# A fused two-block kernel: the order of the second attention's steps, where the last scan's inputs stand, and the order of the W_dt products

## The chip, the cores and the metric

The kernel runs on one core of one Trainium2 chip. The time is the device time of one execution in microseconds (us), the median of three runs. A core has five engines with queues of their own: TensorE (PE: matrix products and transposes into PSUM), VectorE (DVE), ScalarE (ACT), GpSimd (POOL) and SyncE (SP, which here only issues transfers). ACT and POOL issue transfers too. SBUF and PSUM are the core's memories; what does not fit goes through DRAM.

## The reference

Four parts, each added to x, for 4 sequences of 512 tokens of 512 channels: causal attention with 16 heads; a feed-forward layer with ternary weights; a state-space scan; and a block of latent attention with mixture-of-experts. Cut to the parts that the change touches:

```python
x = x + attn0(layernorm(x));  x = x + ternary_ffn(layernorm(x))

u = layernorm(x)                                  # the scan
xz = u @ W_xproj.T                                # delta_r (128), B (16), C (16)
delta = softplus(delta_r @ W_dt.T + b_dt)         # (4, 512, 512)
dA = exp(delta[..., None] * -exp(A_log))          # 16 states per channel
Bu = delta[..., None] * B[:, :, None, :] * u[..., None]
h_t = dA_t * h_{t-1} + Bu_t;   y_t = sum(h_t * C_t, -1)
x = x + y + u * D_param

n = rmsnorm(x, ln1_w)                             # the second attention
kv, qd = n @ kv_d_w, n @ q_d_w                    # latents of 128
k, q, v from kv, qd and rotary parts; 16 heads of 32
probs = softmax(causal(q @ k.T / sqrt(32)))
h = x + (probs @ v) @ o_w
out = h + moe(rmsnorm(h, ln2_w))                  # 7 routed experts, top 2, and a shared one
```

## The kernel before

P = 128 rows is the unit; a sequence b (0 to 3) is four blocks of 128 tokens (NT) and four blocks of 128 channels (NK). The program runs in stages one after the other on the same core: first attention (to about 390 us of the profile), feed-forward (to 755), scan (to 1116), second attention (1163 to 1567, with an entry before it), experts (to the end). Within a stage, work of the next stage is woven in as Python generators, of which each `next` emits one part.

**Feed-forward.** PE's order is written out by hand (`manual_schedule`); the other engines' order is the framework's. For each block of hidden rows PE makes the gate and up products (`pg`, L819) and later the down products (`y`, L837). While sequence b is in the feed-forward, `prepare(b - 1)` makes the scan's inputs of the sequence before. In it, the step size is softplus of a product with W_dt: four products of 128x512 into the tile `pz` (L606), two halves of one PSUM pair each time. ACT reads each for |z| (`e`), DVE for max(z, 0) (`delta`, L608). A half is one part of the generator, so blocks of the feed-forward stand between the halves. The finished `delta`, and `dx` = delta times u turned to rows of tokens, are stored to DRAM (`deltas`, `dxs`).

**Scan.** 128 steps m: for each b, state n (16) and half of the channels. All five engines' orders are written out by hand. `scale(b, n)` loads a diagonal matrix (`diag_l`) on SP's queue, scales three token blocks of dx with B_n on ACT (`bu`, L1016) and makes four exponentials on ACT (`da`, L1022). `turn` forms the transposed inputs in PSUM on PE (L1029, L1034), `scan` runs two 512-long scans on DVE (L1042), `weigh` loads a row of C to all partitions (`cb`, SP's queue) and multiplies on POOL (`hc`, L1053, 128x1024), `add_up` adds up over n on PE (L1066). The pool `large` has two buffers of `delta_l` and `dxT`; `fetch(b)` fills one from DRAM in four parts, each with one load of `dxT` and one of `delta_l` of 256 KB, on SP's queue.

For the last sequence `prepare_last` makes the inputs during the scan itself, one part at each odd step from m = 5; its last parts copy each block on ACT from PSUM to a small tile and store it from ACT's queue. At m = 84 what is left of it is emitted, its pool is closed, and in the room of that pool come tiles for later (`ln2`, `wr`, `br` loaded at once). Then `fetch(B - 1)` starts, one part a step, and from m = 88 one weight load a step is issued from the list `loads` (`ln1`, `wlat`, `wrk` and others). At m = 100, 102, 104, 106 POOL scales a 128x256 block of `wlat` and one of `wrk` by `ln1` (L1164). From m = 86 `come` emits the entry of sequence 0 into the second attention at every third step; its root-mean-square helper is at L102.

**Second attention.** L1382 runs over m, 32 pairs of heads and query blocks for each sequence (b, group g of four heads, query block t, pair p). PE's order is written out, the others' is the framework's. The functions of a step:

- `soften(m)`: scores of two heads on PE (`scd`, L1303, one of two PSUM pairs), causal mask and negated row maximum on DVE (`nm`, L1311), two exponentials with row sums on ACT (`pr`, L1314).
- `turn`: t + 1 transposes for each head on PE (`tpd`, L1326), copied from PSUM by DVE for the first head (`ptd`, L1331) and by ACT for the second (L1333).
- `weigh`: for four heads the product of turned probabilities and values on PE (`avd`, L1344); after the last t, DVE multiplies by the inverted sums.
- `widen_sums`, `invert`: reciprocal on DVE, widened on ACT (`wide`, L1359), four transposes on PE (`tpr`, L1369) and a copy on ACT.
- fillers: parts of `leave` (output projection, residual and norm of the sequence before) and `enter` (latents, projections and rotary parts of the next).

A step emits soften(m), turn(m-2), at even m weigh of the two pairs m-4 and m-3, then fillers.

Of the kernel before, what the change touches and what calls it, by code (L numbers as in the profile page):

```python
# [19 lines left out]
P = 128  # L20
# [26 lines left out]
def block_kernel(ctx: ExitStack, tc: tile.TileContext, a: dict, out: bass.AP):  # L47
# [449 lines left out]
    large = scans.enter_context(tc.tile_pool(name="large", bufs=2, reuse_waits="tile"))  # L497
    loaded = {}

    def fetch(b):  # L500

        delta = large.tile([P, NK, T], F32, tag="one", name="delta_l")
        dxT = large.tile([P, NT, C], F32, tag="two", name="dxT")
        loaded[b] = delta, dxT
        for i in range(NT):
            nc.sync.dma_start(dxT[:, i, :], by_tokens(dxs, b)[:, i, :])
            nc.sync.dma_start(delta[:, i, :], by_rows(deltas[b])[:, i, :])
            yield
# [45 lines left out]
    def prepare(b, pool, spot, spots, ahead):  # L554


        x = xs[b]
        uT = pool.tile([P, NK, T], F32, tag="uT", name="uT")
        ops, rows = [], {}
        layer_norm(pool, x, lambda t, op: ops.append(op))  # L560
        yield

        def make(t):
            row = rows[t] = pool.tile([P, C], F32, tag="row", name="row_s", bufs=ahead)
            ops[t](row)
            ud = pool.tile([P, C], F32, tag="u", name="ud")
            nc.gpsimd.tensor_tensor(ud, row, dpar, ALU.mult)
            nc.gpsimd.tensor_tensor(x[:, t, :], x[:, t, :], ud, ALU.add)

        make(0)  # L570
        make(1)
        yield
        for t in range(NT):
            transpose_into(uT, rows.pop(t), t * P, spot=spot)
            if t == 1:
                make(2)
                make(3)
            yield
        pd = spot("pd")
        for k in range(NK):  # L580
            nc.tensor.matmul(pd, wx[:, k, :RANK], uT[:, k, :], start=k == 0, stop=k == NK - 1)
            if k == 1:
                yield
        drT = pool.tile([P, T], F32, tag="drT", name="drT")
        nc.scalar.copy(drT, pd)
        yield
        pb = spot("pb")
        latents(pb, uT)
        bcT = pool.tile([P, P], F32, tag="bcT", name="bcT")
        nc.scalar.copy(bcT, pb[:, :P])  # L590
        keep_latents(b, bcT, nc.sync)
        yield
        pb = spot("pbt")
        nc.tensor.transpose(pb[:, :P], bcT, ident)
        e = pool.tile([P, NK, T], F32, tag="e", name="diag_s")
        nc.sync.dma_start(diags[b], keep_inputs(b, pb, e))
        yield
        yield


        delta = pool.tile([P, NK, T], F32, tag="delta", name="delta")
        e = pool.tile([P, NK, T], F32, tag="e", name="e")
        for half in range(2):
            for i, pz in enumerate(spots("pz")):
                k = 2 * half + i
                nc.tensor.matmul(pz, wdt[:, k * P : (k + 1) * P], drT, start=True, stop=True)  # L606
                nc.scalar.activation(e[:, k, :], pz, AF.Abs, bias=bdt[:, k : k + 1])
                nc.vector.tensor_scalar(delta[:, k, :], pz, bdt[:, k : k + 1], 0.0, ALU.add, ALU.max)  # L608
            yield half == 1
        nc.scalar.activation(e, e, AF.Exp, scale=-1.0)  # L610
        yield True
        for k in range(NK):
            u = pool.tile([P, T], F32, tag="u", name="u")
            nc.vector.tensor_scalar(u, e[:, k, :], 1.0, -1.0, ALU.add, ALU.add)
            nc.vector.tensor_tensor(u, e[:, k, :], u, ALU.subtract)
            nc.vector.tensor_tensor(delta[:, k, :], delta[:, k, :], u, ALU.add)
            yield True
        nc.scalar.activation(e, e, AF.Ln, bias=1.0)
        yield True
        scaled = {}  # L620

        def finish(k):
            nc.vector.tensor_tensor(delta[:, k, :], delta[:, k, :], e[:, k, :], ALU.add)
            nc.sync.dma_start(deltas[b, k * P : (k + 1) * P, :], delta[:, k, :])
            scaled[k] = pool.tile([P, T], F32, tag="ux", name="ux", bufs=2)
            nc.vector.tensor_tensor(scaled[k], delta[:, k, :], uT[:, k, :], ALU.mult)

        def turn_out(k):
            tp, ux = spot("tpd"), scaled.pop(k)
            for t in range(NT):  # L630
                nc.tensor.transpose(tp[:, t * P : (t + 1) * P], ux[:, t * P : (t + 1) * P], ident)
            st = pool.tile([P, NT, P], F32, tag="st", name="st")
            nc.scalar.copy(st.rearrange("p t q -> p (t q)"), tp)
            nc.sync.dma_start(by_tokens(dxs, b)[:, :, k * P : (k + 1) * P], st)

        finish(0)
        yield True
        finish(1)
        yield
        for k in range(NK):  # L640
            turn_out(k)
            if k + 2 < NK:
                yield True
                finish(k + 2)
            yield

    def prepare_last(b, pool):
# [70 lines left out]
        for t in range(NT + 1):  # L718
            if t > 0:
                nc.vector.tensor_tensor(x[:, t - 1, :], x[:, t - 1, :], y, ALU.add)  # L720
            if t < NT:
                y = bank("du")
                for k in range(NK):
                    nc.tensor.matmul(
                        y[:, k * P : (k + 1) * P], uT[:, k, t * P : (t + 1) * P], dd[:, k, :],
                        start=True, stop=True,
                    )
                yield
        terms = ((ident, relu), (ident, e), (minus, over), (ident, ln))
        scaled = tp = None  # L730
        for k in range(NK + 2):
            if k >= 2:
                st = pool.tile([P, NT, P], F32, tag="st", name="st")
                nc.scalar.copy(st.rearrange("p t q -> p (t q)"), tp)
                nc.scalar.dma_start(by_tokens(dxs, b)[:, :, (k - 2) * P : (k - 1) * P], st)
            if 1 <= k <= NK:
                delta = pool.tile([P, T], F32, tag="delta", name="delta", bufs=2)
                nc.scalar.copy(delta, pd)
                nc.scalar.dma_start(deltas[b, (k - 1) * P : k * P, :], delta)
                scaled = pool.tile([P, T], F32, tag="ux", name="ux", bufs=2)  # L740
                nc.vector.tensor_tensor(scaled, pd, uT[:, k - 1, :], ALU.mult)
            if k < NK:
# [254 lines left out]
    with tc.tile_pool(name="c_1", bufs=1, reuse_waits="tile") as c1, tc.tile_pool(  # L997
# [83 lines left out]
        with tc.manual_schedule(engines=engines):  # L1081
# [4 lines left out]
            for m, (b, n, half) in enumerate(steps):  # L1086
# [27 lines left out]
                if m == 84:  # L1114
# [3 lines left out]

                    far = ctx.enter_context(tc.tile_pool(name="far", bufs=1, side="right"))
                    ln2 = far.tile([P, C], F32, tag="ln2", name="ln2")  # L1120
                    nc.sync.dma_start(ln2, a["ln2_w"].partition_broadcast(P))

                    wr = far.tile([P, NK, RW], F32, tag="wr", name="wr")
                    nc.gpsimd.memset(wr, 0.0)
                    nc.sync.dma_start(wr[:, :, :NR], by_rows(a["router_w"]))
                    br = far.tile([P, NR], F32, tag="br", name="br")
                    nc.sync.dma_start(br, a["router_b"].partition_broadcast(P))
                    logit = far.tile([P, TT, NR], F32, tag="logit", name="logit")

                    hs = [far.tile([P, NT, C], F32, tag=f"h{b}", name=f"h{b}") for b in range(B)]  # L1130
# [22 lines left out]
                    cos1 = held("cos1", [P, NT, RD], a["cos1"].rearrange("(t p) d -> p t d", p=P))  # L1153
                    sin1 = held("sin1", [P, NT, RD], a["sin1"].rearrange("(t p) d -> p t d", p=P))
                    wow = held("wow", [P, NK, C], by_rows(a["o_w"]))
                    coming = fetch(B - 1)
                if m >= 84:
                    next(coming, None)
                if m >= 88 and loads:
                    loads.pop(0)()  # L1160
                if 100 <= m < 100 + 2 * NK and m % 2 == 0:
                    k = (m - 100) // 2
                    for w in (wlat[:, k].rearrange("p i r -> p (i r)"), wrk[:, k]):
                        nc.gpsimd.tensor_scalar(w, w, ln1[:, k : k + 1], None, ALU.mult)  # L1164
            for step in steps[-3:]:
                add_up(*step)
            finish(B - 1)
# [58 lines left out]
    with tc.tile_pool(name="d_1", bufs=1) as d1, tc.tile_pool(name="d_2", bufs=2) as d2, tc.tile_pool(  # L1226
# [68 lines left out]
        def soften(b, g, t, p):  # L1295
# [13 lines left out]
            )  # L1309
            nm = d3.tile([P, 2], F32, tag="nm", name="nm")  # L1310
            nc.vector.tensor_reduce(nm, sc[:, :, :w], AX.X, ALU.max, negate=True)  # L1311
            pr = d3.tile([P, 2, T], F32, tag="pr", name="pr")
            for i in range(2):
                nc.scalar.activation(  # L1314
                    pr[:, i, :w], sc[:, i, :w], AF.Exp, bias=nm[:, i : i + 1],
# [57 lines left out]
        with tc.manual_schedule(engines={mybir.EngineType.PE}):  # L1373
# [2 lines left out]
            left = iter(())  # L1376
            n = len(pairs)
            each = n // B
            for m in range(n + 3):
                b, at = divmod(m, each)  # L1380
                if m < n:
                    soften(*pairs[m])  # L1382
                if 1 <= m < n + 1 and pairs[m - 1][2:] == (NT - 1, 1):
                    widen_sums(*pairs[m - 1][:2])
                if 2 <= m < n + 2:
                    turn(*pairs[m - 2])
                if 2 <= m < n + 2 and pairs[m - 2][2:] == (NT - 1, 1):
                    invert(*pairs[m - 2][:2])
                if m >= 4 and m % 2 == 0:
                    weigh(*pairs[m - 3][:3])  # L1390

                if m == (B - 1) * each:
                    fetch_shared()
                if m >= each and at == 2:
                    left = leave(b - 1, outs[b - 1])
                if at >= 3:
                    next(left, None)
                if at == 7:
                    come = enter(b + 1, d2) if b + 1 < B else iter(())
# [337 lines left out]
```

## Time and profile before

| | us |
|---|---|
| median of three runs | 1910.6 (1908.81 to 1911.85) |
| the profiled execution | 1912.04 |
| its span | 1910.3 |
| feed-forward, 390 to 755: PE busy | 335.1 of 365 |
| scan, 755 to 1116: PE, DVE, ACT, POOL busy | 317.3, 320.4, 308.2, 311.7 of 361 |
| second attention, 1163 to 1567: PE busy | 378.7 of 404 |
| experts, 1567 to 1910: PE busy | 336.1 of 343 |

The profile is one execution; the span goes from its first to its last recorded instruction. A row of the page's fifth part reads: line, engine, operation, output tile <- input tiles, shape, count, then busy time, mean duration in ns of one, and the idle time just before such instructions with what ended it. A row of waits reads: who waited, for whom, us in total, how often, the longest. Names like `SPq` mean an engine's queue of transfers. What a stage is worth is read from its own window, since each has another limit:

```profile
PE   7999999999999988988988888999999999999998
DVE  6456445656564636998979856475565663422222
ACT  2433433333242436989977956566676662111111
POOL 2221212120202020989868940100001000144431
```

These are busy tenths in 40 equal slices of the span, 47.8 us each. The scan is slices 16 to 23, where POOL's row is high.

### The profile page before, as it was taken

The page shows a single profiled execution, that of the slowest core. Times are in us where ns is not written, and L with a number is a line of the kernel's source. Part 1 is how long each engine was busy: PE and PEld are TensorE (multiplying, and loading weights), DVE is VectorE, ACT ScalarE, POOL GpSimd, SP SyncE. Part 2 cuts the span into 40 slices and gives each one's busy share as a digit, 9 for nine tenths or more (in the row PEclk, how much of TensorE's full clock was granted, in tenths as well). Part 3 has the DMA queues.
Part 4 walks back from the last instruction along what each step waited for, and adds up shares of the span by engine and source line. Part 5 has one row for each costly group of instructions (what it writes and reads, how often), then busy time and mean ns, then how long its engine had stood idle before and what let it go on. Part 6 is the DMA issues. An engine that isn't in the chain of part 4 may idle for free. (4 is left out here: it accounts for less than half of the span.)

```text
span 1910.3 us, 27470 instructions
## 1 busy us (share of the span) xinstructions
PE 1767.4 (93%) x10374; PEld 1089.5 (57%) x10374; DVE 1119.4 (59%) x1812; ACT 937.5 (49%) x1932; POOL 575.0 (30%) x391
## 2 busy tenths in 40 slices
PE   7999999999999988988988888999999999999998
PEld 3433343437766666878877764555555554554444
DVE  6456445656564636998979856475565663422222
ACT  2433433333242436989977956566676662111111
POOL 2221212120202020989868940100001000144431
PEclk9999999999999999999999988999999999999999
DMA  7002200102010202332234200000001005545545
GB/s 250 8 1 89 82 1 1 45 1 78 1 56 34 89 23 78 96 112 81 70 127 125 62 6 1 1 10 14 1 23 34 23 7 179 196 89 89 93 81 139
DMA packets 78470, 119.27 MB, mean 62 GB/s; under 512 B 9802, under 2 KB 37066, under 8 KB 77780
## 3 DMA queue, kind: packets, MB, share of 16 engines
q1 hardware_dynamic: 66148, 92.97, 15.1%
q0 software_dynamic: 8656, 20.32, 6.0%
q10 hardware_dynamic: 3536, 4.23, 0.7%
q8 instruction: 83, 1.36, 0.3%
q14 instruction: 47, 0.39, 0.1%
HBM read 85.12 MB, written 35.52 MB: 63 GB/s over the span
## 5 line engine op out<-in xcount | busy, mean ns | idle before, releaser
L1053 POOL TENSOR_TENSOR hc<-h,cb 128x1024 f32<-128x1024 f32 x128 | 301.1, 2406 | 112.6 <-DVE h L1042 94.1
L1042 DVE TENSOR_TENSOR_SCAN h<-da,bu 128x512 f32<-128x512 f32 x256 | 291.2, 1199 | 26.1 <-PE bu L1034 13.1
L284 PE MATMUL pq<-wqkv,hT 128*128 128x512 f32 x384 | 179.4, 615 | 1.8 <-ACT hT L133 1.8
L1022 ACT ACTIVATE da<-delta_l,am 128x511 f32<-128x511 f32 x256 | 163.9, 709 | 6.7 <-DVE h L1042 6.7
L1314 ACT ACTIVATE pr<-scd,nm 128x128 f32<-128x128 f32 (+3 forms) x256 | 133.2, 528 | 56.1 <-DVE nm L1311 53.5
L819 PE MATMUL pg<-hTh,w 128*128 128x512 f32 (+1 forms) x352 | 146.3, 416 | 2.4 <-DVE sil L825 1.7
L1066 PE MATMUL ys<-ident,hc 128*128 128x128 f32 x1024 | 138.6, 279 | 6.9 <-POOL hc L1053 4.0
L819 PE MATMUL pg<-hTl,w 128*128 128x512 f32 (+1 forms) x352 | 140.1, 398 | 0.2 <-DVE hTl L807 0.2
L1034 PE MATMUL bu<-ident,bu 128*128 128x128 f32 x768 | 133.2, 281 | 7.5 <-ACT bu L1016 7.5
L1616 PE MATMUL pgr<-wgu,gTe 128*128 x304 | 137.1, 593 | 0.0
L1016 ACT ACTIVATE bu<-dxT,bts 128x512 f32<-128x512 f32 x192 | 124.3, 711 | 23.1 <-PE bu L1034 21.2
L1029 PE MATMUL bu<-diag_l,dxT 128*128 128x128 f32 x512 | 108.7, 295 | 27.1 <-DVE h L1042 15.3
L364 ACT ACTIVATE pt<-sc 128x1024 f32<-128x1024 f32 (+3 forms) x128 | 84.1, 698 | 85.0 <-PE sc L359 82.6
L284 PEld LDWEIGHTS pq<-wqkv,hT 128*128 128x128 f32 x384 | 71.4, 194 | 94.4 <-issue 84.8
L1066 PEld LDWEIGHTS ys<-ident,hc 128*128 128x128 f32 x1024 | 119.7, 144 | 9.5 <-POOL hc L1053 5.9
L1303 PE MATMUL scd<-qkTd 32*128 32x512 f32 (+3 forms) x512 | 106.9, 496 | 13.7 <-ACT pr L1314 12.7
L1029 PEld LDWEIGHTS bu<-diag_l,dxT 128*128 128x128 f32 x512 | 81.3, 198 | 48.1 <-DVE h L1042 26.9
L1311 DVE TENSOR_REDUCE nm<-scd 128x2 f32<-128x256 f32 (+3 forms) x128 | 104.2, 815 | 0.0
L1326 PEld LDWEIGHTS tpd<-ident,pr 128*128 128x128 f32 x640 | 68.8, 142 | 60.2 <-issue 41.6
L1034 PEld LDWEIGHTS bu<-ident,bu 128*128 128x128 f32 x768 | 96.5, 146 | 11.5 <-ACT bu L1016 11.4
L365 POOL TENSOR_SCALAR_AFFINE_SELECT pt<-pt 128x512 f32<-128x512 f32 x64 | 43.5, 679 | 197.0 <-ACT pt L364 197.0
L1326 PE MATMUL tpd<-ident,pr 128*128 128x128 f32 x640 | 100.3, 288 | 0.6 <-ACT pr L1314 0.6
(310 smaller groups left out, 3184.9 us busy)
## 6 DMA issues: line engine op xcount, KB each, us to landing
cb<-c_rows SPq DMA_DIRECT2D x64, 256.0 KB, 3.1
q_w<-in_w2T SPq DMA_DIRECT2D x20, 256.0 KB, 2.8
delta_l<-deltas SPq DMA_DIRECT2D x16, 256.0 KB, 3.6
dxT<-dxs SPq DMA_DIRECT2D x16, 256.0 KB, 4.2
diag_l<-diags SPq DMA_DIRECT2D x64, 64.0 KB, 1.9
hrows<-h SPq DMA_DIRECT2D x4, 1024.0 KB, 4.6
acc<-x SPq DMA_DIRECT2D x16, 256.0 KB, 2.0
wgu<-in_r_gate SPq DMA_DIRECT2D x7, 512.0 KB, 9.6
```

The costliest lines, as they stand in the source:

```text
L284: nc.tensor.matmul(y, inputs_T[b][:, k, t * P : (t + 1) * P], wqkv[:, k, s * C : (s + 1) * C], start=k == 0, stop=k == NK - 1,)
L819: nc.tensor.matmul(pg[:rows, i, :], w[:, k, f * P : f * P + rows], part[:, k, :], start=k + m == 0, stop=k + m == NK,)
L1016: nc.scalar.activation(row, dxT[:, t, :], AF.Copy, scale=bts[:, b, t * NS + n : t * NS + n + 1])
L1022: nc.scalar.activation(da[:, k, 1:], delta[:, k, 1:], AF.Exp, scale=am[:, k, n : n + 1])
L1029: nc.tensor.matmul(bu[:, :P], loaded[b][1][:, 0, k * P : (k + 1) * P], scaled[b, n][0], start=True, stop=True,)
L1034: nc.tensor.transpose(bu[:, t * P : (t + 1) * P], scaled[b, n][t][:, k * P : (k + 1) * P], ident)
L1042: nc.vector.tensor_tensor_scan(h[:, i, :], decays[b, n][:, 2 * half + i, :], bu, 0.0, ALU.mult, ALU.add)
L1053: nc.gpsimd.tensor_tensor(hc, states.pop((b, n, half)), weighed[b, n].unsqueeze(1).to_broadcast([P, 2, T]), ALU.mult)
L1066: nc.tensor.matmul(sums[b][t][:, k * P : (k + 1) * P], hc[:, i, t * P : (t + 1) * P], ident, is_transpose=True, start=n == 0 and k == 0, s ...
L1314: nc.scalar.activation(pr[:, i, :w], sc[:, i, :w], AF.Exp, bias=nm[:, i : i + 1], accum_out=sums[b, g][:, t, 2 * p + i : 2 * p + i + 1],)
L1326: nc.tensor.transpose(tp[:, j * P : (j + 1) * P], pr[:, i, j * P : (j + 1) * P], ident)
L1616: nc.tensor.matmul(pg, gT[:, k, :], wgu[:, bass.ds(e, 1), k, :].rearrange("p e o -> p (e o)"), start=k == 0, stop=k == NK - 1,)
```

## The change

Three edits.

Second attention: the pair m-3 is turned at the start of step m, ahead of the scores of m (before: m-2, behind them). `invert` comes one step later, `weigh` at odd m from 5 on for the pairs m-5 and m-4, the fillers one step later, and `pr` has a fourth buffer.

Scan: `places(b)` only takes the two tiles of `large`. `prepare_last` takes them for the last sequence and copies from PSUM straight into them; its eight stores and the eight loads of `fetch(B - 1)` are gone. `ln2`, the memset of `wr`, `wr` and `br` move to the end of the list `loads`, which starts at m = 86. The eight scalings by `ln1` go from POOL to ACT, at m = 104 to 110.

Feed-forward: in `prepare` both W_dt products of a half are issued before their readers.

```diff
-    def fetch(b):
-
+    def places(b):
         delta = large.tile([P, NK, T], F32, tag="one", name="delta_l")
         dxT = large.tile([P, NT, C], F32, tag="two", name="dxT")
         loaded[b] = delta, dxT
+        return loaded[b]
+
+    def fetch(b):
+
+        delta, dxT = places(b)
...
         for half in range(2):
-            for i, pz in enumerate(spots("pz")):
+            both = spots("pz")
+            for i, pz in enumerate(both):
                 k = 2 * half + i
                 nc.tensor.matmul(pz, wdt[:, k * P : (k + 1) * P], drT, start=True, stop=True)
+            for i, pz in enumerate(both):
+                k = 2 * half + i
                 nc.scalar.activation(e[:, k, :], pz, AF.Abs, bias=bdt[:, k : k + 1])
...
+        delta, dxT = places(b)
...
             if k >= 2:
-                st = pool.tile([P, NT, P], F32, tag="st", name="st")
-                nc.scalar.copy(st.rearrange("p t q -> p (t q)"), tp)
-                nc.scalar.dma_start(by_tokens(dxs, b)[:, :, (k - 2) * P : (k - 1) * P], st)
+                nc.scalar.copy(
+                    dxT[:, :, (k - 2) * P : (k - 1) * P], tp.rearrange("p (t q) -> p t q", t=NT)
+                )
             if 1 <= k <= NK:
-                delta = pool.tile([P, T], F32, tag="delta", name="delta", bufs=2)
-                nc.scalar.copy(delta, pd)
-                nc.scalar.dma_start(deltas[b, (k - 1) * P : k * P, :], delta)
+                nc.scalar.copy(delta[:, k - 1, :], pd)
...
-                    nc.sync.dma_start(ln2, a["ln2_w"].partition_broadcast(P))
...
-                    nc.gpsimd.memset(wr, 0.0)
-                    nc.sync.dma_start(wr[:, :, :NR], by_rows(a["router_w"]))
...
-                    nc.sync.dma_start(br, a["router_b"].partition_broadcast(P))
...
-                    coming = fetch(B - 1)
-                if m >= 84:
-                    next(coming, None)
-                if m >= 88 and loads:
+                    hold(ln2, a["ln2_w"].partition_broadcast(P))
+                    loads.append(lambda: nc.gpsimd.memset(wr, 0.0))
+                    hold(wr[:, :, :NR], by_rows(a["router_w"]))
+                    hold(br, a["router_b"].partition_broadcast(P))
+                if m >= 86 and loads:
                     loads.pop(0)()
-                if 100 <= m < 100 + 2 * NK and m % 2 == 0:
-                    k = (m - 100) // 2
+                if 104 <= m < 104 + 2 * NK and m % 2 == 0:
+                    k = (m - 104) // 2
                     for w in (wlat[:, k].rearrange("p i r -> p (i r)"), wrk[:, k]):
-                        nc.gpsimd.tensor_scalar(w, w, ln1[:, k : k + 1], None, ALU.mult)
+                        nc.scalar.activation(w, w, AF.Copy, scale=ln1[:, k : k + 1])
...
-            pr = d3.tile([P, 2, T], F32, tag="pr", name="pr")
+            pr = d3.tile([P, 2, T], F32, tag="pr", name="pr", bufs=4)
...
-            for m in range(n + 3):
+            for m in range(n + 4):
                 b, at = divmod(m, each)
+                if 3 <= m < n + 3:
+                    turn(*pairs[m - 3])
                 if m < n:
                     soften(*pairs[m])
                 if 1 <= m < n + 1 and pairs[m - 1][2:] == (NT - 1, 1):
                     widen_sums(*pairs[m - 1][:2])
-                if 2 <= m < n + 2:
-                    turn(*pairs[m - 2])
-                if 2 <= m < n + 2 and pairs[m - 2][2:] == (NT - 1, 1):
-                    invert(*pairs[m - 2][:2])
-                if m >= 4 and m % 2 == 0:
-                    weigh(*pairs[m - 3][:3])
+                if 3 <= m < n + 3 and pairs[m - 3][2:] == (NT - 1, 1):
+                    invert(*pairs[m - 3][:2])
+                if m >= 5 and m % 2 == 1:
+                    weigh(*pairs[m - 4][:3])
...
-                if m >= each and at == 2:
+                if m >= each and at == 3:
                     left = leave(b - 1, outs[b - 1])
-                if at >= 3:
+                if at >= 4:
                     next(left, None)
```

## The prediction

> **What bounds the kernel now.** I read the page's busy shares first, then the four stages as windows (390:755 ternary feed-forward, 755:1116 scan, 1163:1567 second attention, 1567:1910 experts), then in each stage that the change touches PE's waits.
>
> ```profile
> PE 1767.4 (93%) x10374; PEld 1089.5 (57%) x10374; DVE 1119.4 (59%) x1812; ACT 937.5 (49%) x1932; POOL 575.0 (30%) x391
> ```
>
> PE is the bound on average, so only the places where it stands, or is fed at half rate, can give time back.
>
> ```profile
> 390.00:755.00 365.00, 335.11 (x1657) 240.07 (x1650) 206.16 (x321) 136.66 (x198) 49.19 (x42) 0.99 0.14 45
> 755.00:1116.00 361.00, 317.27 (x2461) 282.76 (x2460) 320.44 (x304) 308.18 (x500) 311.71 (x142) 0.96 0.30 92
> 1163.00:1567.00 404.00, 378.68 (x3073) 223.85 (x3072) 251.16 (x519) 260.39 (x794) 20.39 (x17) 0.99 0.04 13
> 1567.00:1910.00 343.00, 336.14 (x1077) 167.59 (x1075) 102.87 (x222) 58.56 (x116) 99.47 (x82) 1.00 0.51 121
> ```
>
> The columns are the stretch, its length, then busy us of PE, PEld, DVE, ACT, POOL, the granted clock, the DMA share and GB/s. PE is idle 29.9 us in the feed-forward and 25.3 us in the attention. In the scan PE, DVE, ACT and POOL are all busy 308 to 320 of 361 us: four co-bound engines, where work moved from one to another gains little, but a stop of all four is lost whole. The experts are untouched.
>
> Feed-forward, PE's waits:
>
> ```profile
> PE pz L606 <- DVE delta L608: 11.5, 6, 3.5
> ```
>
> Two W_dt products go to the two banks of one pair; the second waits each time until DVE has read the first. Six times, 11.5 us.
>
> Scan, window 984:1004, all waits:
>
> ```profile
> PE bu L1029 <- DMA diag_l<-diags: 7.9, 1, 7.9
> DVE h L1042 <- PE bu L1034: 6.7, 2, 6.6
> POOL hc L1053 <- DMA cb<-c_rows: 6.5, 1, 6.5
> POOL wr L1124 <- DMA dxs<-st: 3.5, 1, 3.5
> DVE ux L741 <- ACT delta L738: 1.2, 1, 1.2
> ```
>
> and SP's queue, window 970:1010:
>
> ```profile
> SPq L1121 <- DMA dxs<-st: 15.5, 1, 15.5
> ```
>
> This is m = 84: SP holds the ln2 load until the last dxs store has landed (991.5), then issues ln2, wr, br and the first of eight 256 KB loads ahead of the next diag_l and cb. All four engines stop. Four scan steps take 18.6 us there, against 8.9 to 9.2 in quiet places, which is eight scans of the row below and a little.
>
> ```profile
> L1042 DVE TENSOR_TENSOR_SCAN h<-da,bu 128x512 f32<-128x512 f32 x256 | 291.2, 1199 | 26.1 <-PE bu L1034 13.1
> ```
>
> The other dear place is m = 104 (17.4 us for four steps), window 1044:1066:
>
> ```profile
> L1164 POOL TENSOR_SCALAR wlat<-wlat,ln 128x256 f32<-128x256 f32 x3 | 2.9, 951 | 0.0
> L102 DVE TENSOR_SCALAR ri_rms<-ss_d 128x4 f32<-128x4 f32 x1 | 3.7, 3733 | 2.7 <-ACT sq_d L915 2.7
> ```
>
> POOL spends 0.95 us on each of eight weight scalings, and a 128x4 DVE operation that takes 0.15 to 0.17 us elsewhere takes 3.73.
>
> Attention, PE's waits in 1163:1567, 24.4 us in all:
>
> ```profile
> PE scd L1303 <- ACT pr L1314: 10.6, 23, 0.8
> PE tpr L1369 <- ACT wide L1359: 4.3, 10, 1.2
> ...
> PE tp L132 <- ACT ptd L1333: 1.9, 3, 0.8
> PE tpr L1369 <- DVE ptd L1331: 1.3, 3, 0.4
> ...
> PE tpd L1326 <- ACT pr L1314: 0.6, 1, 0.6
> ```
>
> **Part 1, W_dt side by side.** No instruction is added. PE now issues both products of a half, then eight pg products, and the second half's products wait for the last reader of the first half's pair. From the timeline at 533 to 545: a product is two passes of 0.59 us, 0.43 from start to start, so both take 1.7; eight pg passes, 0.23 apart, 1.8; ACT's e 0.69, DVE's delta 0.75, and ACT's second e waits for the first delta, since both read one pair. Counted from the first product: products and pg until about 3.6 us; e 1.1 to 1.8, d 1.85 to 2.6, e 2.65 to 3.35, d until 4.1. So a new wait of 0.6 us stands at the second pair, where 1.9 us stood at each half on average. The y products behind them start at about 6.3 us instead of 8.6. That is 2.4 us each for the first two of the three batches. For the third, where ACT also stands 2.5 us for a diagonal store, the wait was 3.5 us and the products after it took 0.63 us instead of 0.40 (half clock): 4.3 us. Sum 9.1, I take **9**. Low end 4: ACT, whose new order puts a gated copy ahead of the logarithm for two batches, is late, and every new wait is 1.5 us longer for three batches. High end 14: 11.5, plus 2.5 of slow matmuls.
>
> [...]
>
> **Part 2, the scan.** Removed: eight ACT-queue stores (issue 0.38 us for deltas, 0.33 for dxs, 2.8 us of ACT's sequencer), eight SP loads, and from m = 84 ln2, wr and br. ACT's copies now go straight into the large tiles (same 128x512 shape, 0.57 to 0.59 us). Batch 1 has read its large tiles by m = 63, and the first copy comes at about 67, so that wait is empty. With no store to wait for, SP reaches diag_l and cb of the next step at once, and they land in 1.9 and 3.1 us against a lead of over two steps. The stop goes: 7.9 us PE, with 8.8 us ACT beside it, is one stop, and the four steps fall from 18.6 to about 10.5 (the batch's `finish`, 2.45 us on DVE, is elsewhere; entry work stays). I take **8.1**. Low end 6: the loads of ln1, wlat and others now start at m = 86 and share the queue with diag_l. High end 9.7, the whole excess over 8.9.
>
> The ACT issues stood ahead of DVE's ux (1.2 us, three times in all): **0.5**, between 0 (ACT has other work) and 1.2.
>
> Eight scalings move to ACT at m = 104 to 110. ACT's nearest row is a 128x256 copy of 0.37 us; with 0.71, that of its 128x512 form, above: 3.0 us, up to 5.7. POOL loses 7.6. At m = 104 the excess is about 8.2: DVE waits 2.0 for POOL, 2.7 for ACT's sq_d, and 3.6 in the slow ri_rms. ACT is full from 1030 to 1060, so the 3.0 comes back; 2.0 + 3.6 - 3.0 = 2.6, and ri_rms may still meet one of POOL's products: **2** of the 2.6, from -1 (ACT sets the pace for the eight, 5.7 against 4.7) to 5.
>
> The slow ri_rms ended exactly with POOL's hc, and so did ri_ln (1.93 us at 1021). [...]
>
> New on SP: wr's load (m = 99) waits for POOL's memset behind hc(98), with diag_l and cb of two steps behind it. cb has about 0.3 us to spare; `finish` of the batch covers the rest. Cost 0 to 2, in the low end. Scan sum **10.6**, 5 to 15.
>
> **Part 3, second attention.** Scores, turns and averages are as many as before. On PE the order was scores(m), turn(m-2), averages, filler, scores(m+1); now scores(m), averages, filler, turn(m-2), scores(m+1). Between two scores the same work stands, so the 10.6 us for a free score pair is not moved by order alone. What moves: tpr comes one step (about 2 us in steps without filler) after its widened sums, where its longest wait is 1.2, so 4.3 + 1.3 go, and tpd's 0.6. On DVE the row maximum of odd steps now precedes the copies of turned probabilities, so ACT's exponentials start up to 0.7 us earlier there; I count 2 of the other 12.5 us (pair and ptd waits), since in the fullest steps PE is busy 7.7 of 9.0 us per four and DVE 7.5. Sum **8**; upper end 24, all waits. Lower end -10: the mirror of the gain, copies late behind the maxima (0.815 us by L1311's row) in a fifth of 64 odd steps.
>
> **Sum.** 9 + 10.6 + 8 = 27.6. The profiled span becomes 1910.3 - 27.6 = 1882.7; its run was 1912.0, 1.7 around the span. The median shown is 1910.6, 1.4 under that run: 1883.0.
>
> **Rivals.**
> A. The attention's waits only change places (the same work between two scores speaks for it, the moved tpr against): 0 for part 3, 1891. The same figure stands for another single term lost: part 1 at 4 and a new SP stop of 3.6 at wr.
> B. Attention gains more, 20: exponentials earlier also free score pairs. 1871. Against it: the order between scores is unchanged.
> C. The change does half of what it says: the stop at m = 84 returns at 86 to 100, since the 14 loads go on one queue with diag_l and cb, and the attention stays. Only 9 to 11 remain, 1900.
> D. Slower: on DVE the copies ptd stand behind mask and maximum of newer scores, tpd's banks come free late, and PE stands at turn(m-2) with the next scores behind it. Price 0.815 us at each of 64 odd steps, 52 us when all is bare; it cancels the other 19.6 at 38% and is slower beyond 0.2% at 45%; that the averages read copies made at least one whole step before speaks against it. Half bare, 26: 1910.6 - 19.6 + 26 = 1917.
>
> **Chances.** Forecast (1876 to 1888) 0.45; A 0.24; B 0.12; C 0.10; D 0.09. A measurement tells about 0.2% (3.8 us) from no change. D splits into 0.06 slower and 0.03 within; C gives 0.01 to within: faster 0.90, same 0.04, slower 0.06. The range 1866 to 1900 leaves out D, some of C and the far side of B, less than 2 in 10; the forecast's own is 1876 to 1888.
>
> **What would show it.** Right: no wait of L606's product over 1 us; no all-engine stop near m = 84; POOL without the scalings; tpr without waits; attention some 396 us long. Wrong: PE waiting for ptd or nm in odd steps (D), diag_l or cb as releaser after m = 84 (C), scd<-pr still 10 or more with a length of 404 (A), or ACT the releaser of DVE's scans at 104 to 111.

## The result, and the profile after

The changed kernel takes 1891.0 us (1889.5 to 1894.0, four runs), the kernel before in the same session 1911.2 (1908.8 to 1914.6): a ratio of 0.988 (0.986 to 0.990), 20.2 us faster. The forecast was 1883, in a range of 1866 to 1900; 1891 lies inside the range, but above the 1876 to 1888 that the prediction called its forecast proper. The profiled execution has a span of 1888.5 us.

Its stages as windows, with edges moved to the same instructions (the columns are as before: busy us of PE, PEld, DVE, ACT, POOL, then granted clock, DMA share, GB/s):

```profile
391.00:752.00 361.00, 335.61 (x1657) 241.98 (x1650) 206.19 (x321) 137.09 (x198) 49.65 (x42) 0.98 0.14 45
752.00:1102.00 350.00, 315.90 (x2461) 283.58 (x2459) 318.34 (x304) 310.44 (x508) 304.35 (x134) 0.96 0.28 83
1150.00:1546.00 396.00, 377.64 (x3083) 228.96 (x3076) 257.98 (x519) 260.96 (x797) 20.36 (x17) 0.98 0.04 13
1546.00:1888.00 342.00, 335.91 (x1075) 167.39 (x1073) 102.76 (x222) 58.30 (x115) 99.51 (x82) 1.00 0.51 122
```

PE is as busy as before in every stage, and the stages are shorter mainly by what it no longer waits. For finer accounts I set the start of each PE instruction against that of the same instruction in the trace before (the alignment, below). Between a place ahead of each part and one behind it (514, 800, 1140 and 1567 us of the trace before), the changed trace gains 4.1 us in the feed-forward (the 9 of the forecast), 10.5 in the scan (10.6) and 7.6 in the attention (8). Ahead of all changed code it had lost 1.0, which other executions of the same code gain or lose too. So one term of three is far from its forecast. The last two sums also hold time that the edits did not set, which the section on the prediction takes out.

PE's waits from 430 to 752 show it:

```profile
PE tpd L638 <- DVE ux L633: 6.8, 3, 2.4
PE pz L611 <- DVE delta L615: 4.7, 3, 2.3
```

In the trace before, 514 to 758, the transposes `tpd` waited

```profile
PE tpd L631 <- DVE sil L825: 1.3, 1, 1.3
PE tpd L631 <- DVE ux L626: 1.2, 2, 0.6
```

The products' wait fell from 11.5 to 4.7: 1.2, 1.2 and 2.3 in the three sequences, where the prediction had 0.6 at a pair and, as a sign of being right, none over 1 us. A wait of 6.8 us, 2.2 to 2.4 in each sequence, now stands some 27 us later at the transposes of ux. In the alignment the first of the three sequences gains 2.3 us at the products and loses 3.2 at the transposes (1.6 of that in the stretch at half clock behind the wait, from 562.6: from the start of the transposes to the next `tpf` it is 3.91 us, 2.32 in the trace before); the second gains 2.3 and loses 1.6, the third gains about 4.2 and loses 2.1. That leaves 1.9 of the 4.1; the rest comes from two waits of y for gl between these places, 1.05 and 1.07 us in the trace before, that are missing in this one. E1 and E5 below have one of the two each, so it is not a firm part of the gain.

In the scan the stop at m = 84 is gone: four steps from there take 11.4 us instead of 18.6, the next four 10.5 instead of 12.2. At m = 104, 15.7 instead of 17.4, and DVE's waits from 1030 to 1052 read

```profile
DVE ri_rms L102 <- ACT sq_d L921: 6.7, 1, 6.7
```

so DVE waits for ACT there, where it waited for POOL before. In a window of just those four steps:

```profile
1033.50:1049.20 15.70, 9.71 (x73) 8.42 (x72) 9.05 (x11) 15.64 (x30) 11.78 (x6) 0.94 0.18 61
```

ACT (fourth number) is busy for 15.64 of 15.70 us. PE's waits in the attention, 1150 to 1546:

```profile
PE scd L1306 <- ACT pr L1317: 8.6, 16, 0.7
PE pqd L970 <- ACT pr L1317: 2.5, 3, 0.8
PE tp L132 <- DVE h L1261: 2.5, 3, 0.8
...
PE tpd L1329 <- ACT inv L1374: 0.8, 5, 0.2
```

No wait for widened sums is left; the wait for a free score pair is nearly what it was, in part met by another instruction.

### The profile page after: what moved, and what is told of

Same layout as the page of the kernel before. It is cut to its first block, busy times and chain, and to the rows that moved or that the text cites. A ratio compares the mean times of both kernels' runs of the same rounds, so it can differ in the third digit from the quotient of the medians.

```text
span 1888.5 us, 27478 instructions
## 1 busy us (share of the span) xinstructions
PE 1767.2 (94%) x10374; PEld 1098.3 (58%) x10374; DVE 1123.4 (59%) x1812; ACT 940.1 (50%) x1940; POOL 567.8 (30%) x383
## 5 line engine op out<-in xcount | busy, mean ns | idle before, releaser
L1306 PE MATMUL scd<-qkTd 32*128 32x512 f32 (+3 forms) x512 | 108.3, 504 | 11.1 <-ACT pr L1317 10.7
L1329 PEld LDWEIGHTS tpd<-ident,pr 128*128 128x128 f32 x640 | 74.1, 144 | 36.1 <-issue 22.1
```

What stands on the lines that cost most here:

```text
L1306: nc.tensor.matmul(sc[:, i, :w], qkT[at, g, t * P : w], qkT[at, NG + g, :w], start=True, stop=True)
L1329: nc.tensor.transpose(tp[:, j * P : (j + 1) * P], pr[:, i, j * P : (j + 1) * P], ident)
```

## The experiments

Ratios are to the kernel before, run beside each kernel on the same chip, with 95% intervals. "In its stage" is from the alignment with the trace before, one execution each, between the places named above.

**The parts one by one.** E1 is the kernel before with the W_dt edit only, E2 with the scan's edits only, E3 with the attention's only, each as in the diff above; E9 is the changed kernel without the W_dt edit:

```diff
-            both = spots("pz")
-            for i, pz in enumerate(both):
+            for i, pz in enumerate(spots("pz")):
                 k = 2 * half + i
                 nc.tensor.matmul(pz, wdt[:, k * P : (k + 1) * P], drT, start=True, stop=True)
-            for i, pz in enumerate(both):
-                k = 2 * half + i
```

E1:

> The kernel before with the W_dt products side by side and nothing else. My theory: the two waits at the products go (11.5 us to about 5), but the softplus chain behind them (exponential, four DVE corrections, logarithm, first ux) takes as long as before and was already just in time for PE's transposes tpd, so most of half the gain comes back there: total 4 us faster (2 to 6), with 5 to 8 us of PE waiting for DVE's ux. Rival: the wait at tpd comes from the disturbance by the other two parts (scan loads, pools); then this part alone gains the 9 us of the forecast and PE waits for ux no more than the 1.2 us of before.

1.0004 (0.999 to 1.0017); 3.3 us shorter in its stage. Its PE waits there:

```profile
PE tpd L634 <- DVE ux L629: 6.8, 3, 2.4
PE pz L607 <- DVE delta L611: 4.7, 3, 2.3
```

These are the figures of the changed kernel to a tenth, so the new wait comes from this edit and not from the other parts. The times show no gain at all: at most 1.9 us by the interval, so the 2 to 6 us that I expected in all missed, while the 5 to 8 us of waiting for ux came as expected. In this execution some of the gain is lost in places that the edit doesn't touch, where the granted clock (third number from the right) falls to half for stretches:

```profile
1537.00:1540.00 3.00, 3.00 (x24) 2.07 (x26) 2.12 (x3) 1.37 (x4) 0.00 (x0) 0.50 0.00 0
1540.00:1543.00 3.00, 3.00 (x12) 1.35 (x10) 1.18 (x3) 1.09 (x5) 0.00 (x0) 0.50 0.02 5
1543.00:1546.00 3.00, 3.00 (x24) 2.41 (x28) 2.46 (x5) 2.30 (x6) 0.00 (x0) 0.50 0.00 0
```

From there to 1548 it falls some 3.6 us behind the trace before, in the same instructions.

E2:

> The kernel before with the scan's part alone (last inputs in SBUF, loads moved, scalings on ACT). My theory: parts are independent, 10 to 11 us faster, of which 8 to 9 near m = 84 to 91 and 1 to 2 near m = 104. Rival: part of that gain needs the earlier start or the other order of the feed-forward's stores; then 7 us or less.

0.996 (0.9944 to 0.9977), 7.7 us; 10.3 us shorter in its stage. The steps from 84 take 11.4 us, those from 104 15.7, as in the changed kernel. The stage is as my theory had it. The times allow 4.4 to 10.7 and so cannot tell it from the rival. Part of what is missing in the times can be seen in this trace: the entry behind the scan, 1140 to 1200 of the trace before, takes 4.3 us longer, with eight stretches at half clock in a row where the trace before has five.

E3:

> The kernel before with the second attention's part alone. My theory: 7 to 8 us faster, all between 1163 and 1567, 2.7 us in each of sequences 1 to 3, with PE's waits for widened sums gone and its waits for a free score pair as long as before. Rival: the gain was made by the entry's other timing behind a changed scan; then below 4 us.

0.9937 (0.9916 to 0.9957), 12 us; 8.8 us shorter in its stage. It has the changed kernel's waits, so the gain is the part's own and the rival is out. The times gave more than the 7 to 8 us expected (8.2 to 16.1 by the interval).

E5 is the changed kernel once more, beside E6, E7 and E8:

> The changed kernel unaltered, as the measure for the three beside it. From the parts measured alone (0, -0.4% and -0.63%) the sum is 1.0% faster than the kernel before; from its first measurement 1.2%. A theory in which the parts help each other would give clearly more than 1.0%, one in which they stand in each other's way clearly less.

0.9883 (0.9859 to 0.9907), 1891.5 us. The three parts alone sum to -1.0% and the whole is -1.2%; the intervals are too wide to tell them apart.

E9:

> The changed kernel with the W_dt products in their old order: the scan's and the attention's part together. Alone, the W_dt part gave nothing that the times could show, though its stage was 3.4 us shorter in the profile. If the parts are independent, this kernel is 1.0 to 1.2% faster than the kernel before, the same as the changed kernel within 0.15%. Rival: beside the other parts the W_dt order is worth its 9 us of the forecast; then this kernel is only 0.7% faster.

0.989 (0.9854 to 0.9927), 1894.9 us: the same within the interval. The rival's 0.7% lies just outside it. The W_dt edit by itself is worth somewhere from 0 to 4 us (stages: 1.9 shorter in E5, 3.3 in E1, 4.1 in the first trace after; 1.7 longer in E9 with the old order). From 514 to 745, the six traces with this edit and no further move of the chain (the first after, E1, E5, E6, E8, E11) are 1.3 to 4.1 us shorter than the trace before, and the six with the old order (before, E2, E3, E4, E9, E10) 0.9 shorter to 2.2 longer: 3.1 between the means.

**Where the W_dt gain stays.** E7 gives the softplus chain one part of the feed-forward more:

```diff
         nc.sync.dma_start(diags[b], keep_inputs(b, pb, e))
         yield
-        yield
...
         finish(1)
+        yield
         yield
         for k in range(NK):
```

> The changed kernel, with an empty part taken out ahead of the W_dt products and put ahead of the transposes tpd: the softplus chain gets one part of the feed-forward (about 3 us) more. My theory: PE's waits for ux (6.8 us in the changed kernel) fall below 2 us and the gain of the side-by-side products stays; against it the first half's readers meet the diagonal store of the same tile, which ACT waited 2.5 us for where it was; net 2 to 4 us faster than the changed kernel in the feed-forward. Rival: the chain is bound by DVE's other work there and not by its start, so ux comes no earlier and PE waits for it as long as now.

0.9848 (0.9821 to 0.9876), 1883.8 us against 1891.5 for E5 beside it, and its slowest run (1887.1) is below E5's fastest (1889.1); the feed-forward is 7.7 us shorter than in the trace before, 5.8 more than in E5, which is above the 2 to 4 expected. Its PE waits in that stage:

```profile
PE pz L610 <- DVE delta L614: 4.6, 2, 2.3
PE y L843 <- DVE gl L837: 3.2, 6, 1.2
PE pg L825 <- DVE delta L614: 2.5, 1, 2.5
...
PE tpd L637 <- DVE hTl L813: 1.3, 2, 0.7
```

No wait for ux is left, so the rival is out. The products and the pg behind them wait 7.1 us, because ACT's first e again stands 2.5 us behind the diagonal store of the same tile. That is the price named in the expectation, and it is the smaller one.

E8 issues the corrections of the softplus two to a part:

```diff
             nc.vector.tensor_tensor(delta[:, k, :], delta[:, k, :], u, ALU.add)
-            yield True
+            if k % 2 == 1:
+                yield True
...
         finish(1)
+        yield True
+        yield True
         yield
```

> The changed kernel, with the four DVE corrections of the softplus issued in two parts instead of four, so that the logarithm is issued two parts earlier while the W_dt products and the transposes stay where they are. If the order of issue sets the time of ux, PE's waits for ux fall from 6.8 to under 3 us, and the gated copies behind DVE's corrections may be late instead. If DVE's throughput sets it (DVE is busy without a gap from the end of the exponential to the logarithm), the waits stay at 5 us or more and the time does not change by more than 1 us.

0.9881 (0.9856 to 0.9906), 1890.0 us, and the row of waits is that of the changed kernel:

```profile
PE tpd L639 <- DVE ux L634: 6.8, 3, 2.4
```

The order on ACT is the same instruction for instruction, that on DVE differs at 14 of 1812 places: here, where the framework sets the order, the place of issue in the program hardly moved anything. So this doesn't tell order from throughput, as I had meant it to.

**The scalings.** E4 is E2 with the eight scalings left on POOL:

```diff
-                if 104 <= m < 104 + 2 * NK and m % 2 == 0:
-                    k = (m - 104) // 2
+                if 100 <= m < 100 + 2 * NK and m % 2 == 0:
+                    k = (m - 100) // 2
                     for w in (wlat[:, k].rearrange("p i r -> p (i r)"), wrk[:, k]):
-                        nc.scalar.activation(w, w, AF.Copy, scale=ln1[:, k : k + 1])
+                        nc.gpsimd.tensor_scalar(w, w, ln1[:, k : k + 1], None, ALU.mult)
```

> As the scan's part alone, but the eight scalings by ln1 stay on POOL at m = 100 to 106. My theory: moving them gave only 1 to 2 us, since DVE's root-mean-square helper waits longer for ACT instead of POOL; this kernel is 8.5 to 9.5 us faster than before. Rival 1: the scalings on POOL cost their whole 7 us, so this one gains 4 or less. Rival 2: ACT's extra 4 us cost more than POOL's, so this one is the faster of the two.

0.9969 (0.9948 to 0.9989), 1910.1 us against 1908.4 for E2: a gain of 2.1 to 10 us on the kernel before, too wide to tell the theory from its first rival. So I go by the steps. Those from 104 take 17.4 us, those from 100 9.4 (8.9 in E2), and DVE's rows in 1035:1070 are

```profile
L1045 DVE TENSOR_TENSOR_SCAN h<-da,bu 128x512 f32<-128x512 f32 x23 | 26.2, 1197 | 3.0 <-POOL hc L1056 2.3 <-PE bu L1037 0.7
L102 DVE TENSOR_SCALAR ri_rms<-ss_d 128x4 f32<-128x4 f32 x1 | 4.0, 3974 | 2.5 <-ACT sq_d L918 2.5
```

against these of the changed kernel, 1030:1052:

```profile
L1048 DVE TENSOR_TENSOR_SCAN h<-da,bu 128x512 f32<-128x512 f32 x15 | 16.8, 1190 | 0.0
L102 DVE TENSOR_SCALAR ri_rms<-ss_d 128x4 f32<-128x4 f32 x1 | 0.2, 170 | 6.7 <-ACT sq_d L921 6.7
```

The move took 3.8 us from the operation and gave 4.2 to the wait ahead of it; what was won is the scans' wait for POOL, 2.3 us here and none there.

E6 puts the ACT scalings where ACT had room:

```diff
-                if 104 <= m < 104 + 2 * NK and m % 2 == 0:
-                    k = (m - 104) // 2
+                if 92 <= m < 92 + 2 * NK and m % 2 == 0:
+                    k = (m - 92) // 2
```

> The changed kernel, with the eight scalings by ln1 on ACT at m = 92 to 98 instead of 104 to 110. My theory: at m = 104 ACT became the bound (15.7 of 15.7 us busy for four steps, DVE waiting 6.7 us for sq_d), and at 92 to 99 it has 7 us to spare; the four steps from 104 fall from 15.7 to 12.5 or 13, the steps from 92 to 99 stay at 11.7 each, 2.5 to 3.5 us faster than the changed kernel in the scan. Rival: the weights have not landed by m = 92 (256 and 512 KB loads in one queue with diag_l and cb), ACT waits for them with da and bu queued behind, and the gain is lost there, or worse.

0.9876 (0.9852 to 0.99), 1889.7 us, 1.9 less than E5. The weights were there in time: the steps from 92 stay at 11.7. But those from 104 fell only to 14.9:

```profile
1033.40:1048.30 14.90, 10.15 (x80) 9.11 (x79) 9.25 (x11) 14.84 (x27) 11.52 (x6) 0.93 0.19 62
```

ACT is full there even without the scalings; its wait row for ri_rms reads 5.1 us. The gain that I expected, 2.5 to 3.5 us, was too large: the scan's own exponentials and products with B_n take most of ACT there (15.4 us in its rows of 1033:1050, with those at the edges counted whole), and what the entry adds (h and its squares, 3.3 us) fills the rest. Against E5 the medians differ by no more than the runs of E5 do among themselves.

**The attention.** E10 is the kernel before with `invert` one step later and nothing else:

```diff
-                if 2 <= m < n + 2 and pairs[m - 2][2:] == (NT - 1, 1):
-                    invert(*pairs[m - 2][:2])
+                if 3 <= m < n + 3 and pairs[m - 3][2:] == (NT - 1, 1):
+                    invert(*pairs[m - 3][:2])
```

> The kernel before, with only the transposes of the widened sums (tpr) one step later. My theory: most of the attention's gain is this: PE waits 5.6 us for wide and ptd ahead of tpr in the kernel before; they go, 4 to 6 us faster in 1163 to 1567, 0.2 to 0.3% in the times. Rival: the turn ahead of the scores is what counts; then PE's wait moves on to the next instruction and this kernel gains less than 2 us.

0.9992 (0.997 to 1.0015); 1.7 us shorter in its stage. PE's waits, 1163 to 1567:

```profile
PE scd L1303 <- ACT pr L1314: 10.6, 23, 0.8
PE tp L132 <- ACT qkTd L133: 2.1, 3, 0.7
PE pvd L960 <- ACT qkTd L133: 2.1, 3, 0.7
PE tp L132 <- ACT ptd L1333: 1.6, 3, 0.7
PE tpr L1369 <- DVE ptd L1331: 1.3, 3, 0.4
PE tpr L1369 <- ACT wide L1359: 1.2, 1, 1.2
```

My theory fails. The wait for `wide` goes, but with little for the time; the fillers' own waits (4.2 us for qkTd, 1.6 for ptd) stay, and those are gone in the changed kernel (0.5 and 0.4). By elimination, with E11, most of the gain comes from the turn between the fillers and the scores, together with the averages and fillers that moved one step with it; no run parts these.

E11 takes the fourth buffer of pr away from the changed kernel:

```diff
-            pr = d3.tile([P, 2, T], F32, tag="pr", name="pr", bufs=4)
+            pr = d3.tile([P, 2, T], F32, tag="pr", name="pr")
```

> The changed kernel with three buffers of pr, as before, instead of four. My theory: the pair m-3 is turned ahead of the scores of m, so the buffer is free before the exponentials of m need it: no change, within 1 us in the attention. Rival: ACT waits for the turn in each step, the score pairs come free later, and 3 us or more of the attention's gain are lost.

0.9892 (0.9858 to 0.9926); the attention is 7.4 us shorter than before, against 7.6 with four buffers in the first trace after. So the buffer counts for little or nothing.

**Both moves.** E12 has the edits of E6 and E7:

> The changed kernel with the scalings at m = 92 to 98 and the softplus chain one part earlier, the two moves that were each faster than the changed kernel (1.9 and 7.7 us by their medians). They lie in different stages, so they should add: 1.6 to 1.7% faster than the kernel before, some 1881 us where that takes 1912. Rival: part of the 7.7 us is chance in the clock's half-speed stretches, and the sum is 1.4 to 1.5%.

0.9834 (0.9798 to 0.987), 1884.8 us where the kernel before takes 1913.6. By the medians and ratios it is faster than the kernel before by 28.7 us and than the changed one by 0.5%. In its trace the feed-forward is 7.8 us shorter than before, the scan 12.7 and the attention 8.7. The time is as expected, but the rival's 1.4 to 1.5% lies within the interval too, and whether E12 beats E7 (0.9848) the intervals do not tell.

## Why the prediction was right, and where it was not

The direction and the range held, and so did the mechanism in the scan; the point was 8.0 us too low. In the feed-forward the mechanism stopped one step short, and in the attention the sum was right for another reason than the one given. Of the 27.6 us forecast, the trace after shows 22.2 in the three stages.

**Part 1** failed at one step: "The y products behind them start at about 6.3 us instead of 8.6", from which I booked 9 us. The products do start that much earlier. I followed the chain only to the products' readers and not on to the next place where PE needs it. In the first sequence PE is 2.3 us ahead behind the products, but the last `delta` comes only 0.8 us earlier, and from its end to the transposes (exponential, corrections, logarithm and ux) it is 17.8 us, 17.7 before. So much of what PE gained at the products it waited at the transposes: 6.8 us there, where 2.5 stood before (1.2 for ux, 1.3 for sil). The profile before said so, in a row that I had not priced: PE waited 0.6 us for ux, twice. However short, such a wait means that here the chain came later than PE and had no slack. E1 shows the wait with this edit alone, and E7, with one part more for the chain, reaches 7.7 of the 9.

**Part 2.** The edits show in single groups of four steps, and there the traces agree: in all nine that have the scan's edits whole or with the scalings of E6, the groups from 72, 76, 84, 88 and 100 are 0.54, 0.55, 7.2, 1.66 and 0.28 us shorter than before, to 0.02. With 1.68 from 104 (2.47 in E6 and E12) that is 11.9 for 10.6. The stop at m = 84 went as computed, 7.2 us in its four steps and 1.7 in the next, 8.9 for 8.1. The ACT issues gave 1.1 (72 and 76) for 0.5. The scalings gave 2.0 for 2 (100 and 104), or 2.2 against E4; the forecast's way there was in part another, as one takes 0.50 us on ACT where I took 0.37, ACT became full, and the wait for sq_d grew by 4 us. That the sum over the whole stage is 10.5 comes from two other groups, from 32 and from 108, each 0.7 longer in this trace. Both stand beside stretches at half clock (from 839.1 and 1047.3); the first is as long in E1 and nearly so in E10, without the scan's edits, and the second is not there in E9 and E12, which have them.

The slow ri_rms took 0.17 us once the scalings were gone. That it "may still meet one of POOL's products", for which I took 2 of the 2.6, the run did not show: DVE came to it so late that POOL stood idle, waiting 2.8 us for this very operation, and the wait for ACT had replaced the slow operation. In the trace before it took 3.73 us, began 1.0 us into one hc product and ended within 0.1 us of the end of the next; with the scalings on POOL, in E4, it took 3.97. ri_ln, an operation of the same line and shape, still met an hc product in the trace after: 1.91 us at 1008.8, again ending with it, against 0.15 at 1106.6, where POOL ran nothing. Why it is long there no run shows. Of the new memset ahead of wr's load the trace shows at most one wait of POOL for cb, 0.7 us. The low end of the scan's sum, 5, left out the 0 to 2 set aside for that load; with it the low end was 3.

**Part 3.** 7.6 for 8, but for another reason than given: I had put 5.6 of it on `tpr`, and E10 shows 1.7 for that edit alone. The right total was partly luck. The 7.6 also holds a loss of 1.9 us in the entry, 1140 to 1200 of the trace before, where the changed kernel has eight stretches at half clock in a row instead of five. Behind it, from 1200 to 1567, every one of the nine traces with this part gains 9.3 to 9.5 us. PE's idle time there falls by 6.0 in the trace after (22.6 to 16.6); what makes the rest stays open.

**The rivals.** A was near in its figure (1891), and A gave that figure also to part 1 at 4 together with a new stop at wr's load. Part 1 did give 4.1, but there was no such stop, and the attention, which A had at nothing, kept its gain. C's and D's rows did not appear: no stop for diag_l or cb from m = 84 to 95, and in the attention PE waits 0.4 us for ptd and, in its listed waits, never for nm. ACT as the releaser at m = 104 came half true: it holds up ri_rms and, through it, the scans.

**The clock** was not in the sum at all. Added up over 2 us windows from 390 us on, the time times the missing share of clock is 30.7 us in the trace before and 35.9 in the first trace after; over the other traces it goes from 29.2 to 46.1. Not all of that is on the path, as PE waits anyway in parts of the scan, but it is as large as the terms that I was adding. The 5.4 us between 27.6 and 22.2 can be split by the figures above: part 1 is 4.9 short, the scan's own groups are 1.3 over and the attention behind the entry 1.5 over, and 3.3 were lost beside half-clock stretches, 1.4 in the two groups of the scan and 1.9 in the entry. Why the entry has seven to nine such stretches in eleven traces and five in three (before, E1, E10) stays open.

## What to carry to other kernels

When a wait is removed from an engine, follow the data that it waited for to the next place where the same engine needs something from that chain; here a wait there of 0.6 us in the profile before was the sign that much of the gain would be given back, unless the chain started earlier or the consumer came later. In these traces a wait of over 2 us could cost more than its length: 3.41 us at half clock began with the end of a wait of 2.20 us for ux (below). Work moved from one of several co-bound engines to another is priced by the second engine's load in those very steps, not over the stage. And a total that comes out right doesn't prove its terms: each needs its own run.

## What the runs showed of the hardware

The half-clock stretches come in lumps: in the clock records of all 14 traces each lasts 3.41 us or a multiple of it (but for the one that the end of the trace cuts off), on a grid of 3.41 us that runs through the whole trace, and so costs some 1.7 us (half of it, an estimate) or a multiple if PE has work throughout; behind the first wait for ux it was 1.6. The grid lies differently against the program in each execution, so the stretches fall at different places in the same code. They go with what PE did in the window of the grid just ahead. Of the windows at full clock from 390 us on, in all traces together, all 96 in which PE was busy for less than 40% were followed by one at half clock, 28 of 44 at 40 to 50%, 17 of 106 at 50 to 60%, and 12 of 5597 above that. Taking 60% of 3.41 us, a wait of some 2.1 us was therefore enough (an estimate) when it fell whole into one window, and could pass without a stretch when two windows shared it. The new wait for ux, 2.2 to 2.4 us, is of that length: behind the first of the three, 2.20 us, the changed kernel's trace has a half-clock stretch from 562.6, in which a product of y takes 0.63 us, 0.40 behind it. In the trace before, the products took 0.63 for 0.40 behind the 3.5 us wait (half clock from 705.1) and 0.85 for 0.49 behind the 7.9 us one (from 995.2).

A few stretches have no such sign ahead of them: E1 has three in a row from 1536 in the attention, in instructions that the trace before runs at full clock, though PE was 2.65 of 3.4 us busy in the window just ahead of it (2.45 of 3.00 from 1534 to 1537, where the first begins). So the busy share of one window does not settle it: below 40% a stretch followed each time, above that sometimes, and what else decides no run shows. For traces it means that a difference of 2 to 4 us in a place that an edit doesn't touch and where it moved no wait is not put down to the edit from a single trace, and that stages should be compared instruction by instruction.
